# Two attention layers and an MLP on one core: the order of the opening's bias copy, and the range check and last product at the end

## The chip, the cores and the metric

The kernel runs on one core of a Trainium2 chip. A core has five engines with a queue each: TensorE (PE; matmuls, with the loading of weights shown apart as PEld), VectorE (DVE), ScalarE (ACT), GpSimd (POOL) and SyncE (SP, which here only issues DMA transfers). The metric is the time of one execution on the device in microseconds (us); smaller is better. Line numbers L1 to L1727 are those of the kernel before.

## The reference, cut to what matters

The input x has 16 images of 256 channels by 1024 positions. All of it is float32. Per image:

```python
# layer 0: attention with 4 heads of 64 over the 1024 positions
xs   = x.reshape(B, C, S).transpose(0, 2, 1)
q, k, v = split((xs @ w_proj + b_proj).reshape(B, S, 4, 192), 3, axis=-1)
attn = softmax(einsum('bihd,bjhd->bijh', q, k) * 64 ** -0.5, axis=2)
x    = (einsum('bijh,bjhd->bihd', attn, v).reshape(B, S, 256) @ w_out + b_out + xs).T
# layer 1: 8 heads of 32 on the group norm of x, then an MLP of width 1024
x    = x + attention(group_norm(x, gn1_w, gn1_b), qkv_w, proj_w, proj_b, phys_bias)
h    = gelu(mlp_w1 @ group_norm(x, gn2_w, gn2_b) + mlp_b1)     # exact gelu
out  = x + mlp_w2 @ h + mlp_b2
```

The softmax is taken without subtracting a maximum in the kernel's first pass. So the kernel keeps sums of all denominators and of their inverses, checks at the end that they lie in a safe range, and runs a second, general pass over everything only if they don't. With the inputs of the measurement that second pass isn't run, but its branch is.

## The kernel before, in words

`first_pass` handles the 16 images one after the other, as a software pipeline written out by hand: while the scores of one stage are computed, pieces of its neighbours (the next image's q, k and v, the last image's MLP) are dropped between them, and a small queue, `later`, runs a function so many steps after it was asked for. A scheduler then sets the instructions in order on each engine, with due times of its own; `tc.issue_after(i)` tells it to put what is issued inside behind the instruction i, and `tc.keep_in_program_order` fixes one instruction. Waits between engines are semaphores that the framework adds.

What the change touches, in order of time:

- **The opening** (L1274 to L1298). Three matmuls on a tile of zeros keep TensorE at work (`keep_warm`), the inputs are loaded, and the q, k and v of image 0 are computed, products of two matmuls of 128x512 each (every float32 matmul shows as two records in the trace). The bias of q and k arrives as rows; TensorE turns it (L1282) and VectorE copies the turned bias from PSUM to `bqk` (L1283). ScalarE evacuates each product with that bias (L870). Three PSUM tiles of two banks go round, so the fourth product waits until the first is evacuated. Small preparations are recorded nearby: `exp_bias` (L206, L207: the exponential of a bias on ScalarE, spread by VectorE into `eones`), `scale_v` (L225: the v part of the weights `wq` times `eones`, on VectorE), and on VectorE the averaging matrix `gavg` (L187, L190).
- **Block sums of q and k** (`make_qk_blocks`, L973 to L984): sixteen sums and differences of 128x128 weight blocks, from which later images compute q and k by seven products in place of eight. They are made on VectorE once, in image 0, and stored to DRAM by SP. Their tile is one of a ring of four "e" tiles that the exponentials of the scores use too.
- **The last MLP** (`mlp`, L1088). The 1024 hidden rows are made in eight blocks, as two halves of four; for each block `begin` issues the products 2, 5 and 1, `middle` the products 4 and 3 with two gelus, `finish` the products 7 and 6 with two more. Again seven products stand for eight. `products` lists the seven of the second matrix, and `reduce` issues one: four matmuls, an evacuation or not, and `add_up`, which adds it to the output and issues the store where nothing is missing any more. In the last image product 7 comes last; its `add_up` works in two halves of 256 columns (`num`) after all four matmuls.
- **Tables of ScalarE.** Exp and gelu need different tables. `back_to_exp` issues a one-column Exp after the last gelu of an image, so that the table is loaded early.
- **The range check** (L1423 to L1434): VectorE sums `dsum` and `isum` over columns and compares (L1426, L1427), TensorE counts the partitions in range with a product by ones (L1430), VectorE turns the count into a flag of one element, `in_range` (L1431 to L1434). After the pass, every engine loads that flag (L246) and branches over the general pass (L247).

The lines that the working turns on:

```python
ps, n = bank("bqk", 0), brow.shape[0]                                   # L1281
turn = nc.tensor.transpose(ps[:, :n], brow, ident[:n, :n])
nc.vector.tensor_copy(k["bqk"].rearrange("p t g -> p (t g)"), ps[:, :n])
...
k["exp_bias"]()                                                         # L1291
...
later.after(8, k["scale_v"])
later.after(10, make_qk_blocks)
...
run_pieces(hidden + outputs)                                            # L1420, then the range check
```

Of the kernel before, what the change touches and what calls it, by code (L numbers as in the profile page):

```python
# [14 lines left out]
P = 128  # L15
# [244 lines left out]
def first_pass(ctx, tc, x, out, k):  # L260
# [153 lines left out]
    def attention_a(b, qT, kT, v, project):  # L414
# [26 lines left out]
        def weigh(i, kb, e):  # L441
# [19 lines left out]
            if kb == 1:  # L461
                if c == 0:
                    both[t] = work.tile([P, 2 * CC, TB], F32, tag="es", name=f"es_{key}_{t}", bufs=2)
                sums[i] = both[t][:, 2 * c : 2 * c + 2]
            nc.vector.tensor_add(sums[i], held[i] if kb == 1 else sums[i], e)  # L465
            if kb == SB - 1:
# [75 lines left out]
    def attention_b(b, qT, kT, v, project):  # L542
# [12 lines left out]
        def scores(i, kb):  # L555
            t, c = items[i]
            es = []
            for m in range(2):
# [534 lines left out]
    def mlp(b, xb):  # L1093
# [49 lines left out]
        def finish(i):  # L1143
            if i == n4 - 1 and b >= B - 2:
                later.after(1, back_to_exp)
# [41 lines left out]
        def reduce(number, right, outs, then, part=0, parts=1):  # L1187
# [3 lines left out]
            for i in range(n4):  # L1191
# [3 lines left out]
                )  # L1195
            bias, num, m = None, 1, None
            if len(outs) == 1:
                bias = k["m2b2"]

                num = 2 if b == B - 1 and number == 7 else 1  # L1200
            elif number in (2, 5):
                bias = k["m2b"]
            co = outs[0][0]
            if len(outs) == 2 or "home" in spare:
# [14 lines left out]
                ps = m  # L1219
            assert parts == 1 or m is not None  # L1220

            def add_up():
                for co, t, plus in outs:
                    missing[co, t] -= 1
                    n = TB // num
                    for u in range(num):
                        sl = slice(t * TB + u * n, t * TB + (u + 1) * n)
                        y, p = xb[:, co, sl], ps[:, u * n : (u + 1) * n]
                        if bias is not None:
                            nc.vector.scalar_tensor_tensor(  # L1230
                                y, p, bias[:, co : co + 1], y, ALU.add, ALU.add
                            )
                        else:
                            (nc.vector.tensor_add if plus else nc.vector.tensor_sub)(y, y, p)
                        if not missing[co, t]:
                            nc.sync.dma_start(out[b, co * P : (co + 1) * P, sl], y)
# [45 lines left out]
    turn = nc.tensor.transpose(ps[:, :n], brow, ident[:n, :n])  # L1282
    nc.vector.tensor_copy(k["bqk"].rearrange("p t g -> p (t g)"), ps[:, :n])  # L1283
    tiles0, (first_qk, first_v) = qkv_0(0, xs[0])
# [5 lines left out]
    run_pieces(start[2:])  # L1290
    k["exp_bias"]()  # L1291
    for m in (1, 2):
# [18 lines left out]
    later.after(2, fold_bias)  # L1311
    later.after(8, k["scale_v"])
    later.after(9, k["fold_ones"])
    later.after(10, make_qk_blocks)
    hidden, outputs = [], []
    last = NT * CC * SB // 2 - 1
    for b in range(B):
# [77 lines left out]
        if first:  # L1395
# [19 lines left out]
            fill,  # L1415
        )
        run_pieces(end)
        hidden, outputs = mlp(b, xs[b])
    later.flush()
    run_pieces(hidden + outputs)  # L1420


    ok = small.tile([P, 2], F32, name="ok", bufs=1)  # L1423
    for j, (what, most) in enumerate(((dsum, DEN_MAX), (isum, 1.0 / DEN_MIN))):
        top = small.tile([P, 1], F32, tag="part", name=f"top_{j}")
        nc.vector.tensor_reduce(top, what, AX.X, ALU.add)  # L1426
        nc.vector.tensor_scalar(ok[:, j : j + 1], top, most, None, ALU.is_le)  # L1427

    count = bank("count", 0)[:32, :2]
    nc.tensor.matmul(count, k["ones"], ok, start=True, stop=True)  # L1430
    nc.vector.tensor_scalar(ok[:32], count, P - 0.5, None, ALU.is_ge)  # L1431
    both = small.tile([P, 1], F32, tag="part", name="both")
    nc.vector.tensor_mul(both[:32], ok[:32, 0:1], ok[:32, 1:2])
    nc.vector.tensor_copy(k["in_range"][0:1], both[0:1])  # L1434


# [291 lines left out]
```

## Time and profile before

| what | value |
| --- | --- |
| median of 3 runs | 3623.34 us (3620.74 to 3624.38) |
| the profiled execution's own time | 3623.73 us |
| span of the profiled execution | 3621.7 us |
| TensorE busy | 3588.2 us (99%) |
| VectorE / ScalarE / GpSimd busy | 2781.4 / 2283.7 / 229.9 us |
| mean granted clock of TensorE | 0.998 |
| bytes moved by DMA | 198.30 MB, 55 GB/s on average |

The span runs from the first to the last instruction of the program; the execution's own time has a little more around it. A group of instructions is named by line, engine, operation and "written tile <- read tiles"; the time before `<-` and an engine is idle time and what ended it. Busy TensorE time is partly modelled: [...]the distance between the starts of two records says more than the length of one. The granted clock (PEclk) is the share of full speed that TensorE was allowed.

### The profile page before, as it was taken

The page shows a single profiled execution, that of the slowest core. Times are in us where ns is not written, and L with a number is a line of the kernel's source. Part 1 is how long each engine was busy: PE and PEld are TensorE (multiplying, and loading weights), DVE is VectorE, ACT ScalarE, POOL GpSimd, SP SyncE. Part 2 cuts the span into 40 slices and gives each one's busy share as a digit, 9 for nine tenths or more (in the row PEclk, how much of TensorE's full clock was granted, in tenths as well). Part 3 has the DMA queues.
Part 4 walks back from the last instruction along what each step waited for, and adds up shares of the span by engine and source line. Part 5 has one row for each costly group of instructions (what it writes and reads, how often), then busy time and mean ns, then how long its engine had stood idle before and what let it go on. Part 6 is the DMA issues. An engine that isn't in the chain of part 4 may idle for free.

```text
span 3621.7 us, 81706 instructions
## 1 busy us (share of the span) xinstructions
PE 3588.2 (99%) x35565; PEld 1471.2 (41%) x35565; DVE 2781.4 (77%) x3181; ACT 2283.7 (63%) x3197; POOL 229.9 (6%) x317
## 2 busy tenths in 40 slices
PE   9999999999999999999999999999999999999998
PEld 3434344443443434434344443434434444343433
DVE  5586887868878687876878878688786977868887
ACT  4565757657576674756758566575765757657572
POOL 4000100001000010000000001000010100001000
PEclk9999999999999999999999999999999999999999
DMA  3011221203112131221312213121121212213100
GB/s 129 10 49 39 58 76 37 78 28 68 68 37 75 37 83 45 44 68 39 81 45 52 66 33 81 45 55 63 38 76 45 55 62 48 72 39 65 59 23 23
DMA packets 81572, 198.30 MB, mean 55 GB/s; under 512 B 37974, under 2 KB 38742, under 8 KB 75062
## 3 DMA queue, kind: packets, MB, share of 16 engines
q1 hardware_dynamic: 71828, 164.39, 14.9%
q0 software_dynamic: 7632, 28.21, 5.1%
q8 instruction: 281, 4.60, 0.5%
q14 instruction: 85, 0.70, 0.1%
q10 hardware_dynamic: 1746, 0.40, 0.1%
HBM read 125.85 MB, written 22.27 MB: 41 GB/s over the span
## 4 chain that ended last, share of the span: by engine, by line
PE 81%; DVE 8%; issue 4%; DMA 3%; SPq 2%; ACT 1%; DVEq 0%; ACTq 0%; POOL 0%
PE s_a L428 12%; PE acc_a L451 12%; PE m L1105 10%; PE s_b L569 8%; PE acc_b L621 8%; PE m L357 7%; DVE es_b L595 4%; PE qk_b L1011 3%; PE qk_a L1011 3%; PE v_b L357 3%; PE o L357 3%; PE j L357 3%; PE v_a L357 2%; DMA rd_b<-row_b 2%; PE qk7y_b L1011 1%
## 5 line engine op out<-in xcount | busy, mean ns | idle before, releaser
L582 ACT ACTIVATE e_b<-s_b 128x1024 f32<-128x1024 f32 (+1 forms) x1280 | 982.0, 865 | 137.1 <-PE s_b L569 137.1
L595 DVE TENSOR_TENSOR es_b<-es_b,e_b 128x2048 f32<-128x2048 f32 (+1 forms) x460 | 881.7, 1935 | 101.9 <-ACT e_b L582 85.9
L438 ACT ACTIVATE e_a<-s_a 128x1024 f32<-128x1024 f32 x512 | 520.8, 1024 | 360.2 <-PE s_a L428 357.4
L428 PE MATMUL s_a<-q,k 64*64 64x512 f32 x4096 | 544.3, 593 | 0.0
L451 PE MATMUL acc_a<-e_a,v 64*64 64x512 f32 x4096 | 540.2, 589 | 0.0
L569 PE MATMUL s_b<-q,k 32*64 32x512 f32 x8192 | 527.4, 600 | 4.0 <-DVE res_b L639 2.0
L465 DVE TENSOR_TENSOR es_a<-es_a,e_a 128x1024 f32<-128x1024 f32 x384 | 474.1, 1235 | 69.2 <-ACT e_a L438 49.7
L621 PE MATMUL acc_b<-e_b,v 128*32 128x512 f32 x4096 | 492.1, 598 | 0.0
L357 PE MATMUL m<-g,w 128*32 128x256 f32 (+1 forms) x6456 | 416.6, 385 | 0.0
L357 PEld LDWEIGHTS m<-g,w 128*32 128x32 f32 x6456 | 223.9, 111 | 204.3 <-issue 58.9
L451 PEld LDWEIGHTS acc_a<-e_a,v 64*64 64x64 f32 x4096 | 188.0, 133 | 251.5 <-issue 215.1
L569 PEld LDWEIGHTS s_b<-q,k 32*64 32x64 f32 x8192 | 175.8, 130 | 257.5 <-issue 132.6
L428 PEld LDWEIGHTS s_a<-q,k 64*64 64x64 f32 x4096 | 175.9, 133 | 246.7 <-issue 209.5
L621 PEld LDWEIGHTS acc_b<-e_b,v 128*32 128x32 f32 x4096 | 108.4, 109 | 351.6 <-ACT e_b L582 194.7
L1105 PE MATMUL m<-gn_h,w 128*128 128x512 f32 x512 | 242.3, 601 | 2.9 <-DVE x L1230 1.3
L595 DVE TENSOR_TENSOR es_b<-e_b,e_b 128x2048 f32<-128x2048 f32 (+1 forms) x72 | 147.0, 2051 | 127.8 <-ACT e_b L582 127.8
L1169 DVE TENSOR_TENSOR g<-g,g 128x512 f32<-128x512 f32 (+1 forms) x185 | 195.7, 1069 | 1.2 <-PE m L357 0.8
L1105 PE MATMUL m<-hs,w 128*128 128x512 f32 x384 | 177.9, 592 | 0.1
L1120 ACT ACTIVATE g<-g,m1b 128x512 f32<-128x512 f32 x128 | 91.7, 720 | 110.9 <-DVE g L1149 83.3
L1105 PEld LDWEIGHTS m<-gn_h,w 128*128 128x128 f32 x512 | 93.2, 190 | 118.6 <-issue 100.5
L1120 ACT ACTIVATE g<-m,m1b 128x512 f32<-128x512 f32 x128 | 80.9, 683 | 76.6 <-PE m L1105 76.6
L357 PE MATMUL v_a<-wp,x 128*32 128x256 f32 (+1 forms) x1856 | 121.5, 379 | 0.0
(215 smaller groups left out, 3537.5 us busy)
## 6 DMA issues: line engine op xcount, KB each, us to landing
w<-w_kept SPq DMA_DIRECT2D x30, 1792.0 KB
packed_b<-es_b SPq DMA_DIRECT2D x42, 512.0 KB
packed_b<-es_b POOLq DMA_DIRECT2D x42, 512.0 KB, 6.2
d_a<-row_a SPq DMA_DIRECT2D x64, 256.0 KB
rd_b<-row_b SPq DMA_DIRECT2D x252, 64.0 KB
out_dram<-x SPq DMA_DIRECT2D x63, 256.0 KB
x<-in_x_dram SPq DMA_DIRECT2D x30, 512.0 KB
qk<-qk_kept SPq DMA_DIRECT2D x14, 1024.0 KB
```

The source lines that it names most:

```text
L357: nc.tensor.matmul(o[sl], w[:, sl], r, **flags)
L428: nc.tensor.matmul(s[h : h + HALF, g, :], kT[g * D : (g + 1) * D, c, kb * P + h : kb * P + h + HALF], qT[g * D : (g + 1) * D, c, t * TB : ...
L438: nc.scalar.activation(e, s, AF.Exp, scale=float(D) ** -0.5)
L451: nc.tensor.matmul(accs[i][h][g * D : (g + 1) * D, :], v[h * HALF : (h + 1) * HALF, kb, c * 2 + g], e[h * HALF : (h + 1) * HALF, g, :], st ...
L465: nc.vector.tensor_add(sums[i], held[i] if kb == 1 else sums[i], e)
L569: nc.tensor.matmul(outs[g][h : h + HALF, :], kT[g * D : (g + 1) * D, c, k0 : k0 + HALF], qT[g * D : (g + 1) * D, c, t * TB : (t + 1) * TB] ...
L582: nc.scalar.activation(to, s, AF.Exp, scale=float(D) ** -0.5)
L595: ins = nc.vector.tensor_add(d, (d if kb else es[0][:, g : g + step]), es[m][:, g : g + step])
L621: nc.tensor.matmul(acc[g * D : (g + 1) * D, :], v[:, kb + m, c * G + g], es[m][:, g, :], start=(m == 0), stop=(m == 1),)
L1011: nc.tensor.matmul(to, w, x[right], start=first, stop=True, skip_group_check=not first)
L1105: nc.tensor.matmul(ps, blocks[1][number - 1][:, i * P : (i + 1) * P], inputs[b][number], start=first, stop=True, skip_group_check=not first,)
L1169: (nc.vector.tensor_add if plus else nc.vector.tensor_sub)(d, d, more)
```

## The change

- The copy of the turned bias is kept as `turned`, and `exp_bias` and `scale_v` are issued behind it.
- `make_qk_blocks` writes into a tile of the ring "g" (the MLP's hidden tiles) and not "e"; it is asked for at step 12, not 10, and issued behind the latest sum of exponentials.
- The last Exp of `back_to_exp` is dropped for the last image, and a one-column Gelu (`to_gelu`) is issued behind the last exponential of the last image.
- The range check becomes a function, `check`, issued behind the last `begin` of the last MLP and ahead of its seven last products.
- Product 7 of the last image is issued as two parts of 256 columns, each with its own matmuls, addition and store.

```diff
-            nc.vector.tensor_add(sums[i], held[i] if kb == 1 else sums[i], e)
+            spread_out["es"] = nc.vector.tensor_add(
+                sums[i], held[i] if kb == 1 else sums[i], e
+            )
...
-                        nc.scalar.activation(to, s, AF.Exp, scale=float(D) ** -0.5)
+                        spread_out["exp"] = nc.scalar.activation(
+                            to, s, AF.Exp, scale=float(D) ** -0.5
+                        )
...
-        made = qk_weights(weights_tile("qk7_made"))
+        made = qk_weights(work.tile([P, 4, TB], F32, tag="g", name="qk7_made", bufs=4))
...
-            if i == n4 - 1 and b >= B - 2:
+            if i == n4 - 1 and b == B - 2:
                 later.after(1, back_to_exp)
...
-            bias, num, m = None, 1, None
+            bias, m = None, None
             if len(outs) == 1:
                 bias = k["m2b2"]
-
-                num = 2 if b == B - 1 and number == 7 else 1
...
-            assert parts == 1 or m is not None
+            lo, n = (part * size, size) if m is None and parts > 1 else (0, TB)
 
             def add_up():
                 for co, t, plus in outs:
-                    missing[co, t] -= 1
-                    n = TB // num
-                    for u in range(num):
-                        sl = slice(t * TB + u * n, t * TB + (u + 1) * n)
-                        y, p = xb[:, co, sl], ps[:, u * n : (u + 1) * n]
...
+                    missing[co, t] -= part == parts - 1
+                    sl = slice(t * TB + lo, t * TB + lo + n)
+                    y, p = xb[:, co, sl], ps[:, :n]
...
+                    if not missing[co, t] or lo == 0 and n < TB:
+                        nc.sync.dma_start(out[b, co * P : (co + 1) * P, sl], y)
...
+    def check():
+        ok = small.tile([P, 2], F32, name="ok", bufs=1)
+        for j, (what, most) in enumerate(((dsum, DEN_MAX), (isum, 1.0 / DEN_MIN))):
+            top = small.tile([P, 1], F32, tag="part", name=f"top_{j}")
+            nc.vector.tensor_reduce(top, what, AX.X, ALU.add)
+            nc.vector.tensor_scalar(ok[:, j : j + 1], top, most, None, ALU.is_le)
+        count = bank("count", 0)[:32, :2]
+        nc.tensor.matmul(count, k["ones"], ok, start=True, stop=True)
+        nc.vector.tensor_scalar(ok[:32], count, P - 0.5, None, ALU.is_ge)
+        both = small.tile([P, 1], F32, tag="part", name="both")
+        nc.vector.tensor_mul(both[:32], ok[:32, 0:1], ok[:32, 1:2])
+        nc.vector.tensor_copy(k["in_range"][0:1], both[0:1])
+
+    def to_gelu():
+        one = small.tile([P, 1], F32, tag="part", name="to_gelu")
+        nc.scalar.activation(one, k["ones"][:, :1], AF.Gelu)
...
-    nc.vector.tensor_copy(k["bqk"].rearrange("p t g -> p (t g)"), ps[:, :n])
+    turned = nc.vector.tensor_copy(k["bqk"].rearrange("p t g -> p (t g)"), ps[:, :n])
...
-    k["exp_bias"]()
+    def behind(fn):
+        with tc.issue_after(turned.ins):
+            fn()
+
+    behind(k["exp_bias"])
...
-    later.after(8, k["scale_v"])
+    later.after(8, lambda: behind(k["scale_v"]))
     later.after(9, k["fold_ones"])
-    later.after(10, make_qk_blocks)
+
+    def make_later():
+        with tc.issue_after(spread_out["es"].ins):
+            make_qk_blocks()
+
+    later.after(12, make_later)
...
+        if b == B - 1:
+            with tc.issue_after(spread_out["exp"].ins):
+                to_gelu()
         run_pieces(end)
         hidden, outputs = mlp(b, xs[b])
     later.flush()
-    run_pieces(hidden + outputs)
-
-
-    ok = small.tile([P, 2], F32, name="ok", bufs=1)
-    for j, (what, most) in enumerate(((dsum, DEN_MAX), (isum, 1.0 / DEN_MIN))):
...
+    run_pieces(hidden)
+    with tc.issue_after(mlp_made["begun"].ins):
+        check()
+    run_pieces(outputs[:-1] + [lambda part=part: outputs[-1](part, 2) for part in range(2)])
```

More of the change, by code (lines that the diff above doesn't have):

```diff
@@ L1219, in reduce @@
                 ps = m
-            assert parts == 1 or m is not None
+            lo, n = (part * size, size) if m is None and parts > 1 else (0, TB)
             def add_up():
                 for co, t, plus in outs:
-                    missing[co, t] -= 1
-                    n = TB // num
-                    for u in range(num):
-                        sl = slice(t * TB + u * n, t * TB + (u + 1) * n)
-                        y, p = xb[:, co, sl], ps[:, u * n : (u + 1) * n]
[L1229 to L1236, printed above, removed]
+                    missing[co, t] -= part == parts - 1
+                    sl = slice(t * TB + lo, t * TB + lo + n)
+                    y, p = xb[:, co, sl], ps[:, :n]
+                    if bias is not None:
+                        nc.vector.scalar_tensor_tensor(
+                            y, p, bias[:, co : co + 1], y, ALU.add, ALU.add
+                        )
+                    else:
+                        (nc.vector.tensor_add if plus else nc.vector.tensor_sub)(y, y, p)
+                    if not missing[co, t] or lo == 0 and n < TB:
+                        nc.sync.dma_start(out[b, co * P : (co + 1) * P, sl], y)
                 if then:
@@ L1419, in first_pass @@
     later.flush()
-    run_pieces(hidden + outputs)
-    ok = small.tile([P, 2], F32, name="ok", bufs=1)
-    for j, (what, most) in enumerate(((dsum, DEN_MAX), (isum, 1.0 / DEN_MIN))):
[L1425 to L1434, printed above, removed]
+    run_pieces(hidden)
+    with tc.issue_after(mlp_made["begun"].ins):
+        check()
+    run_pieces(outputs[:-1] + [lambda part=part: outputs[-1](part, 2) for part in range(2)])
 def general_pass(ctx, tc, x, out, k):
```

## The prediction

> **What bounds the kernel now.** I read the page first, then the waits of TensorE (PE), then the opening and the end in order of time. The page's first lines:
>
> ```profile
> span 3621.7 us, 81706 instructions
> PE 3588.2 (99%) x35565; PEld 1471.2 (41%) x35565; DVE 2781.4 (77%) x3181; ACT 2283.7 (63%) x3197; POOL 229.9 (6%) x317
> ```
>
> TensorE is busy for 3588.2 us of 3621.7, so what can be won without removing matmuls is 33.5 us of idle time and any time in which matmuls run slowly. All edits lie in the first 60 us and the last 75 us. The longest single TensorE wait in the list of waits is at the opening (total, times, longest):
>
> ```profile
> PE qk_a L357 <- ACT k L870: 4.8, 1, 4.8
> ```
>
> What stands behind it is seen in VectorE's (DVE) own timeline (start, duration, instruction, idle time before it and its releaser):
>
> ```profile
> 10.22 0.29 DVE L207 COPY eones<-ebias 128x256 f32<-128x256 f32 x1 [8.81 <-ACT ebias L206]
> 14.82 0.76 DVE L225 TENSOR_TENSOR wq<-wq,eones 128x256 f32<-128x256 f32 x2 [4.31 <-DMA wq<-in_L_conv_qkv_w_dram]
> 15.50 0.28 DVE L187 TENSOR_REDUCE borrowed<-borrowed 128x16 f32<-128x128 f32 x1
> 15.69 0.15 DVE L1283 COPY bqk<-bqk 128x6 f32<-128x6 f32 x1
> ```
>
> The copy of the turned bias (L1283) has had its input since 9.92 (the transpose L1282 runs from 9.70 for 0.22), but stands on VectorE behind two products on wq whose weights land at 14.8. ScalarE's (ACT) first k needs the bias, starts at 15.88, and only its end frees a PSUM tile for TensorE at 16.62. The table by stages then shows a second cost (length; PE, PEld, DVE, ACT, POOL busy; PEclk the granted clock; DMA share; GB/s):
>
> ```profile
> 11.60:15.82 4.22, 0.24 (x1) 0.00 (x0) 1.00 (x5) 0.00 (x0) 0.98 (x2) 1.00 1.05 315
> 15.82:22.65 6.83, 6.03 (x7) 2.53 (x8) 0.21 (x2) 2.53 (x4) 3.14 (x5) 0.50 0.56 210
> 22.65:28.29 5.64, 5.64 (x14) 2.47 (x13) 0.00 (x0) 2.06 (x3) 5.62 (x8) 1.00 0.01 1
> ```
>
> About 4 us after TensorE falls idle its clock drops to 0.50 and stays there until 22.65. Seven matmul records start in 6.03 us (0.86 us each) where afterwards 14 take 5.64 (0.40 to 0.43). So the stall costs more than 4.8 us.
>
> At the end, the chain that ended last:
>
> ```profile
> 3579.58 9.71 PE m L1105 x22
> 3589.29 24.10 PE m L357 x56
> 3613.39 0.02 issue
> 3613.41 0.88 DVE x L1230 x2
> 3614.29 0.07 DVE ok L1431
> ...
> 3614.56 0.14 DVE in_range L1434
> ```
>
> The chain stops at the range flag, 7.0 us before the span's end. What fills those 7 us is in the lines of the branch on that flag (L247) and of the program's end (L1724); columns are count, min/median/max ns, first and last start:
>
> ```profile
> L247 PEldq COMPARE_BRANCH  x1: 4115/4115/4115, 3615.3 to 3615.3; - x1
> L247 DVEq EVENT_SEMAPHORE  x1: 21/21/21, 3618.6 to 3618.6; - x1
> L247 PEldq EVENT_SEMAPHORE  x1: 51/51/51, 3619.5 to 3619.5; - x1
> L1724 POOLq DRAIN  x3: 46/107/3743, 3617.2 to 3621.5; - x3
> ```
>
> All five engines load the flag at 3614.7 (0.48 to 0.57 us) and branch; TensorE is through at 3619.5, VectorE at 3618.6; GpSimd (POOL) begins a drain of 3.74 us at 3617.2 only because its branch waited for the flag too, and the last barrier follows at 3620.9.
>
> [...]
>
> **The change, part by part.** I compared how the built program's instructions stand on each engine in both kernels. Between the opening and the last MLP they stand in the same order with the same waits, but for the moved block sums (below).
>
> *Opening.* VectorE's order becomes reduce L187, bias copy, gavg, eones, wq products. No instruction is added. Bias copy at 9.92 + 0.05, to about 10.12. ScalarE still has ebias ahead of the first k; it ran 9.98 to 10.19, when its input landed, so k starts at 10.2 and ends at 10.9. TensorE's third product ends its turn at 11.57 (four records of 0.43 from 9.85), so the freed tile is there 0.6 us early. No wait takes its place: what the next products read of x and wp was issued by 5.2 (the fourth x) and 4.65 (the last wp), and SP and ScalarE pass on to later transfers whose turn needs these landings before 10. So the 20 records run at full clock: 11.57 + 20 x 0.429 = 20.15, where v_a now begins at 28.29. **Gain 8.1 us** (4.8 of stall, 3.3 of half clock). If the clock fell all the same, 4.8; more than 8.2 isn't there. Hidden parts: eones and wq products come later than now only by the 0.5 us of three small instructions, under the wait for wq's landing; folded's DMAs on GpSimd have until the second image.
>
> *Block sums of q and k.* The same 16 VectorE instructions (52.61 to 55.84, 3.2 us) and the same store on SP, two steps later and behind the first sum of item 1 and its res_a addition, in a "g" tile that nobody uses before the first MLP. What is late is the other sums of item 1, by 3.2 us. Cover: VectorE's sum takes 1.2 us of each 1.7 us step, and before the denominators of the first half it has caught up today (idle 0.67 us at 66.1). TensorE has no idle record from 40 to 130. Cost nothing; uncovered, up to 3.2.
>
> *Dummy gelu, no last exp.* The table load (1.28) moves from between L1132 and the first gelu (3569.31) to after an evacuation that ends at 3546.85; ScalarE's next work is at 3553.98, so it is free. The load and dummy at 3592.41 to 3593.9 fall away, ahead of an evacuation nobody waits for. But the order on TensorE changes with it: the product m<-hs of the third hidden block, which stood before the seventh products of the first two, now stands after the third block's first products. Today TensorE stops there:
>
> ```profile
> 3579.58 2.84 PE L1105 MATMUL m<-gn_h,w 128*128 128x512 f32 x6 [0.57 <-DVE g L1150]
> ```
>
> Its records there start at 3578.42 and 3579.58 instead of 3578.85, a hole of 0.73. With the two records (0.86) moved into the hole, the VectorE chain ahead of it (L1149 at 3575.56 to L1150's end at 3579.53) starts 0.86 earlier and the hole is filled: 3579.58 becomes about 3578.8. **Gain 0.8** (0 if gelus hold the earlier products, which are ready 0.2 us ahead; at most 0.9).
>
> *Range check ahead.* The top sums and ok fall into VectorE's idle time at 3584.0 to 3587.6; the count product (two records) stands ahead of the last products: like gm_h's two records at 3557.2, which put 0.14 between neighbours, it costs **0.15**. The three small VectorE instructions after it (0.43) lie among sums read 4 us or more later. SP's load of the flag stands ahead of the fifth-last store, whose data come at 3601.
>
> *Last product in halves and the tail.* Eight records of 0.43 become 16 of 0.216 (v_a's 32 of 256 columns took 6.91 us): no cost. After the last matmul at T, today: VectorE's two halves and three check steps to T + 1.3, load 0.5, [...]TensorE through at T + 6.1, GpSimd's drain to T + 7.5, end at T + 8.3. Then: GpSimd, and ScalarE after its last evacuation at about T - 6, have done all of this long before. TensorE loads the flag at about T - 0.1 and is through 4.1 us after that load: T + 4.5. VectorE has one half (0.48), load (0.57), 3.2: T + 4.4. SP's last store issues at T + 0.55 and lands 1.9 us later, covered. The closing barrier took 0.75 from GpSimd's drain, and SP's last checks 0.25: end T + 5.55. **Gain 2.75**; 1.3 (the check alone) if GpSimd's drain stays last[...].
>
> Sum: 8.1 + 0.8 - 0.15 + 2.75 = 11.5 us of the profiled execution's span of 3621.7, thus 3610.2. That execution took 3623.73, 2.0 beyond its span and 0.4 above the median of the runs, 3623.34. From the median: **3611.8 us**, -0.32%.
>
> **Rivals.**
> - *The tail keeps its length behind the branch.* [...]only the check's 1.3 us go. For: the drain's 3.74 us has no cause in the trace. Against: it starts right after GpSimd's branch and semaphore work. Gain 10.1: 3613.2.
> - *A new wait in the opening.* ScalarE's ebias stands ahead of k and waits for pb (landed 9.97). Up to 10.6 it costs nothing, beyond that one for one. At 13.2 it takes 2.6 back, without a fall of the clock[...]: 3614.4. For: that landing fell among 200 to 360 GB/s of loads. Against: none of these is issued otherwise.
> - *Opening not repaired* (the k evacuations held by another wait): the remainder is 3.4, 3619.9. Against: the order on VectorE and the single wait of k for VectorE.
> - *Slower: the "e" buffers.* The block sums leave the ring of four "e" tiles, so every later user sits one place further. If that broke the overlap of exp, sums and products in each image, TensorE, 99.5% busy between 36 and 3560, couldn't absorb it. From 0.72 us per image (16) it eats the whole gain, from 1.17 us the kernel is slower by over 0.2%; at 1.9, a sum's length, 3642. Against: each tile waits for its fourth predecessor as before, and orders and waits are unchanged.
>
> **How the numbers follow.** The forecast has 0.73, the rivals 0.12, 0.08, 0.04 and 0.03. This kernel's runs spread from 3620.74 to 3624.38, so 0.2% (7.2 us) is about what a measurement of it can tell from no change. The costs' bounds give gains from 8.9 to 12.3; with some 2 us for the medians, 3608.5 to 3616.5, which takes in the first two rivals. Faster by 0.2% is below 3616.1: forecast, first rival, and most of the second, 0.9; within: the rest of it and the third, 0.07; slower: the fourth, 0.03.
>
> **What would show it.** Right: no TensorE wait on k in the opening, clock 1.00 from 5.6 onwards, v_a's first product near 20.2; no hole before the fourth hidden block's products; 5.5 us from the last matmul to the span's end instead of 8.3. Wrong: another releaser near 11.6, half clock anywhere after 6, TensorE idle time between 36 and 3560 other than today's 16.4 us, or GpSimd's long drain still in the last 4 us.

## The result, and the profile after

The changed kernel takes 3613.26 us in the median of ten runs (3610.05 to 3614.79), the kernel before, run beside it, 3622.53 us (3620.69 to 3625.02): a ratio of 0.9973, 95% interval 0.9966 to 0.9981. That is 9.3 us by the medians. The profiled execution is the fastest of the ten, 3610.05 us, so its span, 3608.0 us, flatters the change by some 3 us against the median.

The page of the kernel after begins:

```profile
span 3608.0 us, 81721 instructions
PE 3584.1 (99%) x35573; PEld 1470.7 (41%) x35573; DVE 2780.1 (77%) x3181; ACT 2282.7 (63%) x3196; POOL 232.0 (6%) x317
```

TensorE has eight records more than before (the halves) and 4.1 us less busy time, though no matmul was removed: before, the records at half clock counted as busy for longer, by some 3.0 us (the run warm_stall below). TensorE's own time line in the opening (start, duration, instruction, count) has no gap and no wait for k any more:

```profile
9.40 0.22 PE L1299 MATMUL bqk<-borrowed 6*128 6x6 f32 x1
9.56 10.57 PE L357 MATMUL qk_a<-x,wp 128*128 128x512 f32 x24
19.96 7.07 PE L357 MATMUL v_a<-wp,x 128*128 128x256 f32 x32
```

VectorE's shows why: the copy of the turned bias stands where its input is ready, and the wait of 3.63 us for wq's landing now has nothing behind it that is needed soon.

```profile
5.29 0.29 DVE L187 TENSOR_REDUCE borrowed<-borrowed 128x16 f32<-128x128 f32 x1 [3.88 <-POOL borrowed masks.py:199]
9.66 0.17 DVE L1300 COPY bqk<-bqk 128x6 f32<-128x6 f32 x1 [4.09 <-PE bqk L1299]
9.74 0.22 DVE L190 TENSOR_SCALAR gavg<-borrowed 128x128 f32<-128x128 f32 x1
10.32 0.29 DVE L207 COPY eones<-ebias 128x256 f32<-128x256 f32 x1 [0.35 <-ACT ebias L206]
14.24 0.76 DVE L225 TENSOR_TENSOR wq<-wq,eones 128x256 f32<-128x256 f32 x2 [3.63 <-DMA wq<-in_L_conv_qkv_w_dram]
```

In the table by stages (length; PE, PEld, DVE, ACT, POOL busy; granted clock; DMA share; GB/s) the two stretches that had lost the time are full, at clock 1.00:

```profile
11.60:15.82 4.22, 4.22 (x11) 1.86 (x10) 0.76 (x2) 2.04 (x3) 0.98 (x2) 1.00 1.06 296
15.82:20.20 4.38, 4.38 (x13) 1.96 (x12) 0.00 (x0) 1.41 (x3) 1.73 (x4) 1.00 0.85 328
```

At the end, the chain of work for the last 58 us has one unbroken piece of 50 matmul records where the kernel before had 8.87 and 9.71 us with a VectorE and ScalarE chain between, and stops at the last addition, not at the flag:

```profile
3556.97 21.78 PE m L1109 x50
3578.75 0.15 PE count L1280 x2
3578.90 24.26 PE m L357 x64
3603.17 0.02 issue
3603.19 0.48 DVE x L1230
```

And the lines of the branch on the flag and of the program's end (count, min/median/max ns, first and last start) show the engines passing one by one, and GpSimd's long drain, the first of its three, 21 us before the end:

```profile
L247 PEldq COMPARE_BRANCH  x1: 4075/4075/4075, 3599.3 to 3599.3; - x1
L247 PEldq EVENT_SEMAPHORE  x1: 51/51/51, 3603.4 to 3603.4; - x1
L247 DVEq COMPARE_BRANCH  x1: 72/72/72, 3603.8 to 3603.8; - x1
L247 DVEq EVENT_SEMAPHORE  x1: 21/21/21, 3606.9 to 3606.9; - x1
L1741 POOLq DRAIN  x3: 46/107/3743, 3586.5 to 3607.7; - x3
```

The last matmul ends at 3603.15, the program at 3608.01.

One thing is worse than before. Among TensorE's waits in image 0 (total, times, longest) there is one that the kernel before does not have:

```profile
PE s_a L428 <- DVE res_a L472: 0.7, 1, 0.7
```

The table below cuts every profiled execution of this study into the same stretches, in us: from the first product of q and k to the first v (the 32 records that need no other input than the first loads, x, wp and the bias); image 0, from its first scores to those of image 1; from there to the last image's first scores; and from the last matmul's end to the program's end. The stretches left out (the first loads, v of image 0, the last image) are told where they matter.

| kernel | opening | image 0 | images 1 to 14 | tail | span |
| --- | --- | --- | --- | --- | --- |
| before | 22.11 | 185.40 | 3122.96 | 8.37 | 3621.7 |
| open_only | 14.09 | 192.26 | 3122.08 | 8.37 | 3620.2 |
| qk_only | 20.21 | 185.38 | 3121.83 | 8.37 | 3618.8 |
| end_only | 22.22 | 185.39 | 3122.58 | 4.97 | 3617.0 |
| warm_stall | 20.44 | 185.38 | 3122.35 | 8.36 | 3619.0 |
| after | 14.08 | 186.15 | 3120.86 | 4.86 | 3608.0 |
| after_again | 14.08 | 185.90 | 3123.03 | 4.97 | 3610.7 |
| all_but_qk | 14.80 | 188.54 | 3122.03 | 4.85 | 3612.4 |
| e_tile_new_place | 14.08 | 187.34 | 3121.16 | 4.83 | 3609.6 |
| g_tile_old_place | 20.47 | 185.39 | 3122.26 | 4.90 | 3615.9 |
| qk_at_24 | 14.46 | 185.40 | 3121.78 | 4.86 | 3609.4 |
| late_flag | 14.79 | 186.50 | 3125.58 | 7.60 | 3616.3 |
| no_gelu | 14.08 | 185.91 | 3121.80 | 4.83 | 3610.0 |
| whole_7 | 14.19 | 186.16 | 3122.79 | 4.81 | 3609.8 |

Images 1 to 14, where no kernel here changes anything, move by about 2 us from execution to execution (once by 4.7, in late_flag, where the granted clock fell to 0.50 for 3.41 us; see the last section). So a single span tells little under 2 us, while opening, image 0 and tail can be read from one trace to some tenths. From before to after: opening 8.0, image 0 -0.75, images 1 to 14 2.1 (chance: in the changed kernel's second profile, after_again, it is -0.1), last image 0.55, tail 3.5, and 0.3 because the first loads landed earlier in this execution: 13.7, the difference of the spans.

### The profile page after: what moved, and what is told of

It is laid out like the page before. It is cut to its first block, busy times and chain, and to the rows that moved or that the text cites. A ratio compares the mean times of both kernels' runs of the same rounds, so it can differ in the third digit from the quotient of the medians.

```text
span 3608.0 us, 81721 instructions
## 1 busy us (share of the span) xinstructions
PE 3584.1 (99%) x35573; PEld 1470.7 (41%) x35573; DVE 2780.1 (77%) x3181; ACT 2282.7 (63%) x3196; POOL 232.0 (6%) x317
## 4 chain that ended last, share of the span: by engine, by line
PE 80%; DVE 10%; issue 5%; DMA 3%; SPq 2%; ACT 1%; DVEq 0%; POOL 0%
PE s_a L428 12%; PE acc_a L451 12%; PE m L1109 10%; PE s_b L571 8%; PE acc_b L625 7%; PE m L357 6%; DVE es_b L599 5%; PE qk_b L1015 3%; PE qk_a L1015 3%; PE v_b L357 3%; PE o L357 3%; PE j L357 3%; PE v_a L357 2%; DMA rd_b<-row_b 2%; PE qk7y_b L1015 1%
## 5 line engine op out<-in xcount | busy, mean ns | idle before, releaser
L357 PE MATMUL m<-g,w 128*32 128x256 f32 (+2 forms) x6464 | 416.6, 385 | 0.0
L357 PEld LDWEIGHTS m<-g,w 128*32 128x32 f32 (+1 forms) x6464 | 224.2, 111 | 203.8 <-issue 57.7
```

The costliest lines, as they stand in the source:

```text
L357: nc.tensor.matmul(o[sl], w[:, sl], r, **flags)
```

## The experiments

In the expectations below, a step is one tile of scores, and an item is the eight steps of one pair of heads and one half of the positions, so that layer 0 of an image has the items 0 to 3. v_a, s_a and res_a are the first layer's v, scores and attention result.

**The parts alone, and all but one.** Four kernels were timed in five rounds beside the kernel before (3622.07 us, 49 runs). The first is the kernel before with the order of the opening alone:

```diff
-    nc.vector.tensor_copy(k["bqk"]..., ps[:, :n])
+    turned = nc.vector.tensor_copy(k["bqk"]..., ps[:, :n])
...
-    k["exp_bias"]()
+    behind(k["exp_bias"])               # issue_after(turned)
...
-    later.after(8, k["scale_v"])
+    later.after(8, lambda: behind(k["scale_v"]))
```

> The kernel before with the opening's order alone: bias copy first, eones and the wq products behind it. Block sums and end as before. Theory 1 (the parts add up, the images between are untouched): 8.3 us off, as the trace of the changed kernel has v_a at 19.96 instead of 28.29, so about 3614.2 from 3622.5. Theory 2 (the images between give some 3 us back when they start 8 us earlier, because the whole change measured 9.3 while opening and end in its trace sum to 12.6): about 5 us off, 3617.5.

Measured: 3622.32 us, ratio 1.0000 (0.9992 to 1.0009). The stall on k is gone and the opening is 14.09 us, 8.0 less than in the kernel before's profile; and image 0 takes 192.26 us, 6.9 more. Its waits in image 0 are, first TensorE's, then ScalarE's own line with the idle time before it in brackets:

```profile
PE s_a L428 <- ACT e_a L438: 3.6, 1, 3.6
```

```profile
50.67 1.02 ACT L438 ACTIVATE e_a<-s_a 128x1024 f32<-128x1024 f32 x1 [0.69 <-PE s_a L428]
57.46 1.94 ACT L438 ACTIVATE e_a<-s_a 128x1024 f32<-128x1024 f32 x2 [5.77 <-DMA qk_kept<-qk_made]
```

An exponential needs the e tile in which the block sums of q and k were made, and that tile is free only when their store has landed. SP issues the store at 50.78, 1.9 us after GpSimd's store of 1792 KB at 48.89, and ScalarE goes on at 57.46. In the kernel before the store is issued at 55.95, later still, but the pipeline also comes by later, and no wait is seen. So the opening's gain ran into the next late thing, a store whose time is set by transfers and by GpSimd, and not by TensorE: GpSimd's store lands at 54.91, and the DMA engines are at work until 56.76, 6.0 us after SP's issue. In the kernel before, where GpSimd's packets end at 56.20, 0.25 us after SP's issue, they are done at 59.45, 3.5 us after it. TensorE stands idle for 3.65 us, from 54.89 to 58.54, and the stages around that (columns as above) show that its clock falls to half as well, which makes up most of the rest of the 6.9 us:

```profile
54.00:58.00 4.00, 0.89 (x12) 0.01 (x2) 3.41 (x3) 0.54 (x1) 0.00 (x0) 0.98 0.63 262
58.00:62.00 4.00, 3.46 (x16) 1.03 (x20) 2.45 (x2) 2.43 (x3) 0.00 (x0) 0.50 0.01 4
62.00:66.00 4.00, 4.00 (x32) 1.30 (x28) 0.94 (x1) 1.61 (x2) 0.00 (x0) 0.67 0.00 0
```

The second has the move of the block sums alone:

```diff
-        made = qk_weights(weights_tile("qk7_made"))               # ring "e"
+        made = qk_weights(work.tile([P, 4, TB], F32, tag="g", name="qk7_made", bufs=4))
...
-    later.after(10, make_qk_blocks)
+    later.after(12, make_later)         # issue_after(spread_out["es"])
```

> The kernel before with the block sums alone moved: into a g tile, two steps later, behind the first sum of item 1 and its res_a addition. Theory 1 (hidden, as forecast): within 1 us of before. Theory 2 (the moved sums hold the other sums of item 1 up until TensorE waits, 0.7 us in the trace of the changed kernel on res_a L472): 0.7 us slower. Theory 3 (the block sums' place is where the whole change loses its 3 us): 3 us slower.

Measured: 3623.45 us, ratio 1.0004 (0.9996 to 1.0012). Image 0 takes 185.38, as before: the move costs nothing where the opening stays as late as it was. Its stall on k, 4.3 us, is there.

The third has the edits of the end alone (check ahead, product 7 in halves, dummy gelu):

```diff
-            if i == n4 - 1 and b >= B - 2:
+            if i == n4 - 1 and b == B - 2:
...
-    run_pieces(hidden + outputs)
-    # then the range check
+    run_pieces(hidden)
+    with tc.issue_after(mlp_made["begun"].ins):
+        check()
+    run_pieces(outputs[:-1] + [lambda part=part: outputs[-1](part, 2) for part in range(2)])
```

> The kernel before with the end alone: range check ahead of the last products, product 7 in halves, dummy gelu, no last exp. Theory 1 (parts add up): the hole before the fourth hidden block is filled (0.8), the count product costs 0.15, and the last matmul stands 4.8 us ahead of the end of the span instead of 8.3 (3.5): 4.1 us off, 3618.4. Theory 2 (tail as I priced it, 2.75): 3.4 off. Theory 3 (tail gives the check alone): 2 off.

Measured: 3618.44 us, ratio 0.9990 (0.9981 to 0.9998), 3.6 us less; in the trace the tail is 4.97 us and the last image 0.5 us shorter.

The fourth is the changed kernel with the block sums back in the e ring and at the old step:

```diff
-        made = qk_weights(work.tile([P, 4, TB], F32, tag="g", name="qk7_made", bufs=4))
+        made = qk_weights(weights_tile("qk7_made"))
...
-    later.after(12, make_later)
+    later.after(10, make_qk_blocks)
```

> The changed kernel with the block sums back in an e tile at step 10. Theory 1 (block sums cost nothing): like the changed kernel, 9.3 us off, 3613.2. Theory 2 (0.7 us of wait on res_a in image 0): 10 off. Theory 3 (the block sums' place costs the 3 us): 12.5 off, 3610.

Measured: 3616.84 us, ratio 0.9985 (0.9979 to 0.9992), 5.2 us less than before, against 9.3 for the whole change. ScalarE waits 5.0 us for the store, TensorE 2.9 us for ScalarE, and image 0 takes 188.54. The clock stays at 1.00 this time. The opening is 14.80 us and not 14.08: pb, the input of ebias, lands later in this execution, ebias runs from 11.22, ScalarE's first k stands behind it, and TensorE waits 0.24 us for k. This is the forecast's second rival, in small. The three parts alone come to 0, +1.4 and -3.6, about -2 us; together they make -9.3. So the edit that the forecast priced at nothing lets the opening's gain through to the end. For the last kernel the times alone say so only weakly, as the intervals (2.9 to 7.6 us, and 6.9 to 12.3 for the whole change) touch; the traces give it 2.4 us in image 0 (188.54 against 186.15).

**Tile or place.** The changed kernel with the sums at the new place, but in the e ring:

```diff
-        made = qk_weights(work.tile([P, 4, TB], F32, tag="g", name="qk7_made", bufs=4))
+        made = qk_weights(weights_tile("qk7_made"))
```

> The changed kernel, with the block sums of q and k at their new place (two steps later, behind the first sum of item 1) but in a tile of the e ring as before. Theory (the e tile is held until the store of the sums has landed, in absolute time near 57, so the opening's gain runs into it): ScalarE's exp waits for the store, as it did with the old place (5.0 us, TensorE 2.9 us), here about the same or up to 3 us more because the sums stand later; first s_a of image 0 to first s_a of image 1 188.5 to 191 us instead of 186.15. Rival (the place does it, the tile does not matter): no exp waits for the store, image 0 takes 186.2 us.

Measured in one profile: image 0 takes 187.34 us, and TensorE's and ScalarE's waits in it show the store again (total, times, longest):

```profile
PE s_a L428 <- ACT e_a L438: 1.7, 1, 1.7
```

```profile
ACT e_a L438 <- DMA qk_kept<-qk_made: 3.8, 1, 3.8
```

So the tile is what holds the pipeline, as the theory had it, but the size was expected too high. The sums came 1.1 us later and their store with them, but the e tile was also asked for two places later in the ring: ScalarE's stop comes behind the exponential of 53.42, not behind that of 50.65, and most of the store's time had passed by then.

The other way round, the sums in the g tile but asked for at the old step and with nothing to stand behind:

```diff
-    later.after(12, make_later)
+    later.after(10, make_qk_blocks)
```

> The changed kernel with the block sums in a g tile, but asked for at the old step and with nothing to stand behind. The planned order then puts all 16 sums at the head of VectorE's queue, ahead of the reduce and the turned bias, because the g tile is free from the start. Theory (a copy behind work on late weights stalls TensorE, whatever that work is): wq lands near 14.2, eight sums of 0.2 us and the reduce follow, k ends near 17, TensorE waits 5 to 6 us for k, the clock falls, first v_a at 28 to 30; image 0 without the wait for res_a or for the store, 185.4 us. Rival (the sums find the weights landed earlier, or the wait ends by the clock): v_a below 24.

Measured in one profile: the opening is 20.47 us, the first v at 27.16 (expected 28 to 30: the wait for k is 4.4 us, and half clock lasts only 3.41 us), image 0 185.39. VectorE's time line:

```profile
14.03 0.29 DVE L984 TENSOR_TENSOR qk_made<-wq 128x128 f32<-128x128 f32 x1 [3.42 <-DMA wq<-in_L_conv_qkv_w_dram]
...
15.66 0.28 DVE L187 TENSOR_REDUCE borrowed<-borrowed 128x16 f32<-128x128 f32 x1
15.85 0.15 DVE L1300 COPY bqk<-bqk 128x6 f32<-128x6 f32 x1
```

A g tile is free from the start, so the planned order puts the sums at the head of the queue, where they wait for wq, and the bias copy is late again, behind other work on the same weights. Tile and place belong together: the tile takes the store off the exponentials, the place keeps the sums from stalling the opening.

**Does the half clock follow from the stall?** The kernel before with six more small matmuls on the tile of zeros, three of them behind the third product:

```diff
-    run_pieces(start[2:])
+    run_pieces(start[2:3])
+    keep_warm(nothing, 6)
+    run_pieces(start[3:])
```

> The kernel before, with six small matmuls on a constant tile that feed nothing, three of them behind the third product, in the opening's idle stretch. The wait for k stays about 4.8 us, but the idle stretch stays under 4 us. Theory (half clock is a consequence of the idle stretch and worth 3.3 us of the 8.1): clock 1.00 in all stages from 5.6 on, the 20 records to the first v_a in about 8.6 us after k instead of 10.5 to 11.8, v_a first near 25, where the kernel before has 26.5 to 28.3. Rival (the half clock has another cause, the start of the program or the load traffic): the clock still falls to 0.50 and v_a starts at 26.5 or later.

Measured in one profile: the clock is 1.00 throughout, as the table by stages of this kernel shows.

```profile
11.60:15.80 4.20, 4.20 (x11) 1.76 (x10) 0.32 (x1) 0.00 (x0) 0.98 (x2) 1.00 1.02 298
15.80:22.00 6.20, 5.49 (x14) 2.25 (x13) 0.94 (x5) 3.22 (x5) 2.45 (x5) 1.00 0.68 258
```

From the fourth product's start (17.55) to the first v (26.23) are 8.7 us, where the kernel before needs 11.7 (16.62 to 28.29): the half clock is worth 3.0 us there, and it goes when the idle stretch is filled (what is left of the wait for k is 0.71 us). That v starts at 26.23 and not near 25 is because wq landed later in this execution: VectorE's products on it start at 15.48 instead of 14.82. By the same 20 records it costs 1.6 us in qk_only and 2.4 in end_only (10.29 and 11.07 us against 8.68), so its price changes from execution to execution. The last section has how long half clock lasted in each.

**Why the tail is shorter than forecast.** The changed kernel with the last step of the check behind the last addition:

```diff
-        nc.vector.tensor_copy(k["in_range"][0:1], both[0:1])
+        return lambda: nc.vector.tensor_copy(k["in_range"][0:1], both[0:1])
...
-        check()
+        flag = check()
...
+    with tc.issue_after(made["added"].ins):     # the last addition
+        flag()
```

> The changed kernel, with the last step of the range check (the copy that writes the flag) behind the last addition on VectorE; count, sums and comparison stay where they are. Theory (the tail is short because all engines but VectorE and SP load the flag and branch while TensorE's last matmuls run): from the last matmul's end T to the end of the program 7.0 to 8.0 us instead of 4.8, with TensorE's branch from about T + 1.2 to T + 5.3 and GpSimd's drain of 3.7 us again in the last 5 us. Rival (only the check's own 1.3 us of VectorE work counted, and the halves): T + 5.0.

Measured in one profile: the last matmul ends at T = 3608.68, the program at T + 7.6. All engines load the flag at 3609.3 to 3609.6 again, and GpSimd's drain of 3.74 us is again near the end.

```profile
L247 PEldq COMPARE_BRANCH  x1: 4125/4125/4125, 3609.9 to 3609.9; - x1
L247 PEldq EVENT_SEMAPHORE  x1: 51/51/51, 3614.1 to 3614.1; - x1
L1743 POOLq DRAIN  x3: 46/107/3743, 3611.7 to 3616.0; - x3
```

So of the 3.5 us by which the tail shrank, 2.7 hang on when the flag is there, and the other 0.8 goes with the VectorE work of the check itself, which no run here tests alone.

The changed kernel with product 7 in one piece:

```diff
-    run_pieces(outputs[:-1] + [lambda part=part: outputs[-1](part, 2) for part in range(2)])
+    run_pieces(outputs)
```

> The changed kernel with the last product in one piece: 8 matmuls of 512 columns instead of 16 of 256, one addition of 0.75 us and one store of twice the size. Theory (VectorE's addition, flag load and branch end last): the product takes the same 3.45 us on TensorE, the addition ends 0.27 us later, so last matmul to the end of the program 5.1 us instead of 4.8; the addition of the first half no longer lies beside the matmuls, nothing else changes. Rival (TensorE's branch or the last store ends last): 4.8 us, or 6 us if the larger store lands after VectorE's branch.

Measured in one profile: T + 4.81; the theory's 5.1 is missed. The flag's loads and VectorE's branch show why (T = 3605.03 here):

```profile
L246 PEldq TENSOR_LOAD <-in_range x1: 485/485/485, 3597.2 to 3597.2; - x1
L246 DVEq TENSOR_LOAD <-in_range x1: 540/540/540, 3605.1 to 3605.1; - x1
L247 DVEq COMPARE_BRANCH  x1: 72/72/72, 3605.7 to 3605.7; - x1
L247 DVEq EVENT_SEMAPHORE  x1: 21/21/21, 3608.7 to 3608.7; - x1
```

VectorE's last addition runs from 3605.07 for 0.75 us, until 3605.82, yet its sequencer has loaded the flag and begins its branch at 3605.7: it does not wait for the addition to end. An addition half as long therefore gains nothing, and the halves of product 7 are worth nothing that a trace shows here.

**The hole ahead of the fourth hidden block.** The changed kernel without the early gelu:

```diff
-            if i == n4 - 1 and b == B - 2:
+            if i == n4 - 1 and b >= B - 2:
...
-        if b == B - 1:
-            with tc.issue_after(spread_out["exp"].ins):
-                to_gelu()
```

> The changed kernel without the early dummy gelu, and with the product of the third hidden block, and the return to exp, in the order of before. Theory (the order of TensorE's products filled the hole ahead of the fourth hidden block, worth 0.8 us): a wait of about 0.7 us on VectorE's g stands again ahead of the fourth hidden block, and from the start of gn_h to the end of the last matmul 52.5 us instead of 51.8; a ScalarE table load stands between the last reduce and the first gelu, and costs TensorE nothing or up to 0.3. Rival (the hole closed for another reason, as the count product now takes its place): no hole, 51.8.

Measured in one profile: in TensorE's time line of this kernel it stops there again,

```profile
3571.02 2.84 PE L1109 MATMUL m<-gn_h,w 128*128 128x512 f32 x6 [0.57 <-DVE g L1154]
```

and from the last image's first scores to the last matmul's end it takes 270.08 us where the changed kernel takes 269.18, 0.9 more (0.7 expected). The table load (1.28 us in the traces of before and after) stands ahead of the first gelu, at 3560.75, in idle time of ScalarE. In the changed kernel the same place has no wait, as two records of the third hidden block (m<-hs) now stand in it:

```profile
3566.52 1.93 PE L1109 MATMUL m<-gn_h,w 128*128 128x512 f32 x4
3568.28 1.02 PE L1109 MATMUL m<-hs,w 128*128 128x512 f32 x2
```

So the order of products that came with the dummy gelu fills the hole.

**The wait that the change brings, and a later place.** The changed kernel with `later.after(24, make_later)`, timed in five rounds beside the changed kernel itself:

```diff
-    later.after(12, make_later)
+    later.after(24, make_later)
```

> The changed kernel, with the block sums of q and k twelve steps later still (just behind the third sum of item 2, after the first pair of denominators), in the g tile. Theory (the 0.75 us that image 0 costs is VectorE's backlog of some 4.8 us from the sums, of which 1.6 us is their slowing beside GpSimd's sums of w2, so that res_a, which frees the tile for the next scores, is 0.7 us late at the denominators): at the new place GpSimd's sums are over, the 16 sums take 3.2 us, the backlog has 20 us to go, the wait of s_a for res_a is gone and image 0 takes 185.4 us; the time 0.7 us below the changed kernel's, about half of what five rounds can tell. Rival (image 0 is longer for the stretch's earlier start against GpSimd and the transfers, whatever VectorE does): 186.1 us and a wait of 0.7 us on another releaser.

> The changed kernel itself, beside the one with later block sums. About 3613 us, ratio 0.9975 to the kernel before; first v_a near 20 to 20.5, image 0 185.9 to 186.5 us, tail 4.8 us from the last matmul's end.

Measured, beside the kernel before at 3622.82 us (21 runs): with the later place 3613.59 us, ratio 0.9975 (0.9965 to 0.9985); the changed kernel 3614.64 us, ratio 0.9977 (0.9969 to 0.9986). The 1.05 us between them can't be told from nothing by the times. The traces do tell: image 0 takes 185.40 us, as before the change, and the wait of s_a for res_a is gone, as the theory had it; the changed kernel again takes 185.90, with that wait at 0.4. At the later place GpSimd's sums are over, and the 16 sums take 0.28 us each, from 68.20 to 71.52. What it avoids is seen in VectorE's time line of the changed kernel (first fence), beside GpSimd's of the same microseconds (second):

```profile
44.05 1.91 DVE L465 TENSOR_TENSOR es_a<-e_a 128x1024 f32<-128x1024 f32 x1 [1.66 <-ACT e_a L438]
...
46.48 0.77 DVE L984 TENSOR_TENSOR qk_made<-wp 128x128 f32<-128x128 f32 x1
47.17 0.28 DVE L986 TENSOR_TENSOR qk_made<-wp 128x128 f32<-128x128 f32 x1
47.37 1.36 DVE L985 TENSOR_TENSOR qk_made<-qk_made,wp 128x128 f32<-128x128 f32 x1
```

```profile
47.17 1.41 POOL L157 TENSOR_TENSOR w_made<-w_made 128x512 f32<-128x512 f32 x1
```

VectorE's 128x128 sum of 47.37 takes 1.36 us beside GpSimd's of 1.41 us, where the sums behind it take 0.28 each; it ends at 48.73, when GpSimd's has ended at 48.58. The larger one of 44.05 takes 1.91 us, where the same sum takes 1.23 at 59.03 in qk_at_24. Not every sum is longer: the one of 47.17 starts with GpSimd's and takes 0.28. What makes the others longer is not shown here.

## Why the prediction was right, step by step

The forecast was 3611.8 us, range 3608.5 to 3616.5; measured 3613.26. Its mechanisms hold, two of its terms were mis-sized, and one step was wrong in what it said of a cost. That the total fits so well is in part luck: the tail gave 0.75 us more than forecast, and image 0 cost 0.75 that was put at nothing. The measured time is also that of the first rival, 3613.2, whose mechanism the traces refute.

- **Opening, "Gain 8.1 us".** In the two profiles the opening shrinks from 22.11 to 14.08 us: 8.0. First v at 19.96 (forecast "near 20.2"), clock 1.00, no other releaser. Its split, 4.8 of stall and 3.3 of half clock, is confirmed by warm_stall, with 3.0 for the clock. But 8.1 was read from one profile, and both parts vary: in the three profiled kernels that leave the opening alone (before, qk_only, end_only) the wait for k is 4.8, 4.3 and 5.3 us, as wq lands at other times, and half clock lasts 6.8, 3.4 and 6.8 us. Their openings take 22.11, 20.21 and 22.22 us, 7.4 more than the 14.08 of the changed kernel in the mean, so that is a fairer size, and probably part of why the median gained 9.3 and not 11.5.
- **Block sums, "Cost nothing; uncovered, up to 3.2".** This is the step that failed, in two ways. The move is not a by-work that must not cost anything: without it open_only gains nothing, and the changed kernel keeps 5.2 of its 9.3 us. The forecast asked whether the sums would be late for others, and took the e ring to go on as before; it did not ask what in the next 30 us was timed by transfers and not by TensorE, and so would not move forward with it. And the cost was not nothing, but 0.5 to 1.1 us in the five profiles with this place and tile (185.90 to 186.50 for image 0, against 185.39), 0.75 in the middle of them: the cover (0.49 us of VectorE's idle time per step) was worked out with sums of 0.2 us each, while GpSimd's sums, which stay where they are in time, now fall on them. qk_only, where they don't, shows the cover to be enough.
- **Dummy gelu, "Gain 0.8", and the count, "0.15".** The hole is gone and comes back without the early gelu; the count product took 0.15 in the chain. Together 0.55 in the last image, forecast 0.65.
- **Last product in halves, "no cost".** Right, and no gain either (whole_7).
- **Tail, "Gain 2.75".** Measured 3.5; T + 4.86 where T + 5.55 was expected. The mechanism (flag early, GpSimd's drain out of the way) is right; the term that was mis-sized is when the flag is loaded. The forecast has TensorE load it "at about T - 0.1"; it does so at 3598.70, T - 4.45, and its branch of 4.08 us is over 0.27 us after T. VectorE, which then is last, loads it at T + 0.05, with its last addition and not behind it. The forecast put the load behind the addition; in after the addition runs from 3603.19 for 0.48 us and the load starts at 3603.20, and in whole_7 the branch begins at 3605.7 and the addition ends at 3605.82.
- **TensorE's idle time in the middle.** "Other than today's 16.4 us" was to show it wrong; over the same work, which now lies between 27.67 and 3550.3, it was 15.6 us, with the new 0.7 of image 0 in it. So the total hid a new wait, because other waits vary by more (16.9 us in after_again), and it was no good sign.
- **The rivals.** The tail kept nothing of its length; ebias ended at 10.29, so no new wait arose in this opening, though one of 0.24 us did in all_but_qk, where ebias began at 11.22; the stall was repaired. The slower rival had the e ring as its place, and expected harm from taking the sums out of it; the runs show the reverse, harm from leaving them in.

By the trace's own sizes the sum is 7.4 + 3.5 + 0.55 - 0.75 = 10.7 us; the interval of the ratio, 6.9 to 12.3 us, holds it.

## What to carry to other kernels

When a stall is taken out, list what in the stages behind it is timed by transfers or by an engine that does not follow the stalled one, and whose buffers are tight: those things do not move forward, and they take the gain back at the first place where they hold a tile. Test parts alone and all but one, since a part that is worth nothing alone can carry the rest. And at a branch, ask when the sequencer reaches the load of the condition, not when the engine finishes: a condition that is ready a few microseconds before the last matmul hides TensorE's branch behind the matmuls (here the load began 4.45 us before the last matmul's end, and the branch was over 0.27 us after it). VectorE's stayed in view here: its sequencer reaches the load only with its last addition, and it is through 3.8 us after the last matmul.

## What the runs showed of the hardware

- TensorE begins to load the flag 7.87 us before the last matmul's end in whole_7, where the last records take 0.43 us each, and 4.4 to 4.5 us before it in the other eight profiles whose flag is early, where the last 16 take 0.216. In after, 17 matmul records start behind the beginning of that load.
- TensorE's branch took 4.02 to 4.18 us in the five profiles where all engines branched within 0.7 us (before, open_only, qk_only, warm_stall, late_flag) and 3.48 to 4.14 in the nine whose flag is early: 4.08 in after, where the time from ScalarE's branch to its next record overlapped it by 0.3 us, and 3.75 in whole_7, where that time lay within it. From VectorE's branch to its next record it was 3.24 and 3.36 us in before and late_flag, against 3.08 and 3.04 in after and whole_7. What a branch waits for is not shown. In after, packets of 8 KB of the queue that the page calls "q14 instruction" start 0.95, 0.93 and 1.25 us after the branches of ScalarE, TensorE and VectorE.
- GpSimd's drain at the end took 3.74 us in each of nine profiles. In before, open_only and late_flag it is near the end, in after, whole_7 and g_tile_old_place it starts 21 us or more ahead of it. What it waits for stays open.

The clock takes more room. It is not lost by the length of a pause alone. In before, a wait of 4.8 us was followed by a granted clock of 0.50 for 6.83 us, in end_only one of 5.3 us by 6.8 us of it, in qk_only and g_tile_old_place one of 4.3 and 4.4 us by 3.4 us each, and in open_only a pause of 3.65 us by 6.8 us. One of 2.93 us in all_but_qk left the clock at 1.00. But in late_flag it fell after 3.41 us with 1.44 us of TensorE work in them, so 1.97 us of idle time, and in warm_stall 1.45 us of work in 3.41 us left it at 1.00. The columns below are those of the table by stages; the first three lines are late_flag, the last two warm_stall:

```profile
2206.05:2209.46 3.41, 1.44 (x16) 0.29 (x12) 1.03 (x2) 1.90 (x3) 0.00 (x0) 1.00 0.02 5
2209.46:2212.88 3.42, 3.42 (x20) 0.87 (x16) 3.32 (x3) 0.00 (x0) 0.00 (x0) 0.50 0.20 77
2212.88:2216.29 3.41, 3.41 (x44) 0.90 (x40) 2.34 (x3) 2.57 (x5) 0.00 (x0) 1.00 0.00 0
871.80:875.21 3.41, 1.45 (x16) 0.24 (x8) 0.64 (x2) 2.19 (x3) 0.00 (x0) 1.00 0.10 30
875.21:878.62 3.41, 3.31 (x40) 1.02 (x44) 3.31 (x4) 0.46 (x1) 0.00 (x0) 1.00 0.20 77
```

What decides it is not shown by these runs. The way back took different times too: in before TensorE worked from 16.62 until the clock was 1.00 again at 22.65, 6.0 us, and in late_flag half clock lasted 3.4 us, with TensorE busy for all of it. So what a pause costs in half clock has to be read from the trace of that execution.
